# Two decoder convolutions moved under the pool, by pixel place, in column tiles; joint-step borders moved from TensorE to VectorE

## The chip, the cores and the metric

The kernel runs on one core of a Trainium2 chip. The metric is the device time of one execution in microseconds; before the change it is 17384.9 us, the median of three runs (17384.59 to 17401.33). A core has TensorE (PE, matmuls, with its weight loads shown as PEld), VectorE (DVE), ScalarE (ACT), GpSimd (POOL) and SyncE (SP), which here only issues transfers. Matmuls write to PSUM; the other tiles lie in SBUF.

## The reference, cut to what matters

A network of four residual layers on x of shape (16, 32, 128, 128) in float32. The change lies in the last one, of which this is the part that matters:

```python
def conv3x3(x, w, b): ...            # 32 -> 32 channels, zero padding 1
def maxpool2(x):
    b, c, h, w = x.shape
    return x.reshape(b, c, h // 2, 2, w // 2, 2).max(axis=(3, 5))
def deconv2x2(x, w, b): ...          # each pixel becomes a square of 2x2
orig = x
y = get_operator(x)                  # five normalised edge filters
y = conv3x3(y, conv1_w, conv1_b)     # 128x128
y = maxpool2(y)                      # 64x64
y = conv3x3(y, conv2_w, conv2_b)
y = maxpool2(y)                      # 32x32
y = conv3x3(y, conv3_w, conv3_b)
y = maxpool2(y)                      # 16x16
y = conv3x3(y, conv4_w, conv4_b)
y = deconv2x2(y, deconv1_w, deconv1_b)   # 32x32
y = conv3x3(y, conv5_w, conv5_b)
y = deconv2x2(y, deconv2_w, deconv2_b)   # 64x64
y = conv3x3(y, conv6_w, conv6_b)
y = deconv2x2(y, deconv3_w, deconv3_b)   # 128x128
y = conv3x3(y, conv7_w, conv7_b)
return orig * y
```

The layer's input is a group norm of x, and its result is added to x.

## The kernel before

The layers run one after another. The last stage is `layer3_net`; it finds the output of convolution 1, already half pooled, in DRAM (`p1`). The sixteen images form four groups; the 128 partitions hold four images of 32 channels.

**Setup.** For each of the pairs (deconvolution, convolution) 5, 6 and 7 the weights of one joint step are multiplied out on PE: `W` for the four places (phases) of a 2x2 square, a bias, and the border corrections `edge` (matmuls `pr` at L1943, then short VectorE work on one partition, L1944 to L1954). The buffers for weights are single, so a round's loads wait for the round before.

**Front of a group** (`front`). Eight loads `pt` (512 KB each, two buffers) bring p1; VectorE takes the maximum of two rows (L2053), ScalarE writes it into the padded c2 (L2055). `conv_pool` does convolutions 2 and 3: for a strip of rows nine matmuls with weights that are block diagonal over the four images (`conv9`, L354, 128 rows by 128 columns by 512 pixels) accumulate in one PSUM tile, VectorE takes the maximum over 2x2 (L1969), ScalarE adds the bias and writes the strip (L1973). Convolution 4 is one such step of 256 pixels; its result d1 goes through joint steps 5 and 6 to d2 and d3.

**Joint step.** `windows` loads, with 16 transfers from SP, one tile per image whose four groups of 32 partitions hold the same picture shifted by 0 or 1 in each direction. A matmul of 128 rows and 32 columns per image then yields one phase; the four images lie in four column tiles of PE. Joint 5 reads w5 tiles (36 KB a transfer), joint 6 w6 tiles (136 KB), joint 7 w7 tiles (528 KB). `phase` adds the border corrections with matmuls of one row: the column at L2019, and for a first or last row the row at L2025 and the corner at L2028.

**Output loop of a group.** Joint 7 for eight slices: a slice is 2048 pixels per partition. SP loads xs (1 MB), ScalarE makes xn (L2081), PE four phases, VectorE multiplies (L2088, four times) and adds xs (L2089), and ScalarE's queue stores the slice (1 MB, L2090). xs and xn have two buffers each.

The loop over groups builds the front of the next group ahead of the output loop of the current one. The order on each engine is not the program's: a scheduler fixes it at build time, engine by engine, by the expected readiness of each instruction. As built, PE runs front 0, front 1, output loop 0, front 2, output loop 1, front 3, output loops 2 and 3. SP loads w7 of a group as soon as both its d3 is written and the loop before has read the old w7; `pt` loads of the next group lie in between. The pool of PSUM tiles has seven buffers. SP's transfers carry one of eight semaphores in turn, and a transfer waits for the earlier one with the same semaphore.

Of the kernel before, what the change touches and what calls it, by code (L numbers as in the profile page):

```python
# [10 lines left out]
F32 = mybir.dt.float32  # L11
AF = mybir.ActivationFunctionType
ALU = mybir.AluOpType
AX = mybir.AxisListType
# [3 lines left out]
P = 128  # L18
B, T, HW = 16, 32, 128
# [12 lines left out]
def load(nc, pool, ap, tag):  # L32
    t = pool.tile(list(ap.shape), F32, name=tag, tag=tag)
    nc.sync.dma_start(t, ap)
    return t
# [314 lines left out]
def conv9(nc, ps, wt, src, r0, nr, nw):  # L350

    for t in range(9):
        dy, dx = divmod(t, 3)
        nc.tensor.matmul(  # L354
            ps, wt[:, t], src[:, r0 + dy : r0 + dy + nr, dx : dx + nw],
            start=(t == 0), stop=(t == 8),
        )
# [1534 lines left out]
def layer3_net(tc, w, x3, p1, out, sb3, b3, groups=range(NG)):  # L1892
# [4 lines left out]
    nc = tc.nc  # L1897
    with ExitStack() as ctx:
        cp = ctx.enter_context(tc.tile_pool(name="fc", bufs=1))
        psum = ctx.enter_context(tc.tile_pool(name="fp", bufs=7, space=PSUM))  # L1900
        psw = ctx.enter_context(tc.tile_pool(name="fpw", bufs=1, space=PSUM))
        wc = {i: load(nc, cp, w[f"c{i}_w"], f"c{i}_w") for i in range(2, 5)}
        bb = load(nc, cp, w["l3_b"], "l3_b")
        one = cp.tile([1, 64], F32, name="one", tag="one")
        nc.vector.memset(one, 1.0)


        pairs = {
            (0, 0): [(0, 1)], (0, 1): [(1, 0), (2, 1)],
# [3 lines left out]
        with tc.tile_pool(name="fw", bufs=1) as tp:  # L1913
            for i, k in ((1, 5), (2, 6), (3, 7)):
                wd = load(nc, tp, w[f"d{i}_t"], "d_t")
                bd = load(nc, tp, w[f"d{i}_b"], "d_b")
                wk = load(nc, tp, w[f"c{k}_t"], "c_t")
                pw = psw.tile([P, 4, T], F32, name="pw", tag="pw")
                for s in range(4):
                    first = True  # L1920
                    for ph in range(4):
                        rows, cls = pairs[ph // 2, s // 2], pairs[ph % 2, s % 2]
                        todo = [(dy, dx, p, q) for dy, p in rows for dx, q in cls]
                        for n, (dy, dx, p, q) in enumerate(todo):
                            nc.tensor.matmul(
                                pw[32 * s : 32 * s + 32, ph], wd[:, 2 * p + q],
                                wk[:, 3 * dy + dx, 0:T], start=first, stop=n == len(todo) - 1,
                                tile_position=(0, 32 * s), skip_group_check=True,
                            )
                            first = False  # L1930
                W = cp.tile([P, 4, T], F32, name=f"W{k}", tag=f"W{k}")
                nc.vector.tensor_copy(W, pw)

                pb = psw.tile([P, 4, T], F32, name="pb", tag="pw")
                for t in range(9):
                    nc.tensor.matmul(pb[:, 0, 0:1], wk[:, t], bd, start=(t == 0), stop=(t == 8))
                bias = cp.tile([P, 1], F32, name=f"B{k}", tag=f"B{k}")
                nc.vector.tensor_add(bias, pb[:, 0, 0:1], bb[:, k - 2 : k - 1])

                row = tp.tile([1, 3, 3, P], F32, name="row", tag="row")  # L1940
                for dy in range(3):
                    pr = psw.tile([1, 3, P], F32, name="pr", tag="pw")
                    nc.tensor.matmul(pr, bd, wk[:, 3 * dy : 3 * dy + 3], start=True, stop=True)  # L1943
                    nc.vector.tensor_scalar_mul(row[:, dy], pr, -1.0)  # L1944
                edge = cp.tile([1, 8, P], F32, name=f"E{k}", tag=f"E{k}")
                for a in range(2):
                    nc.vector.tensor_add(edge[:, a], row[:, 2 * a, 0], row[:, 2 * a, 1])
                    nc.vector.tensor_add(edge[:, a], edge[:, a], row[:, 2 * a, 2])
                    nc.vector.tensor_add(edge[:, 2 + a], row[:, 0, 2 * a], row[:, 1, 2 * a])
                    nc.vector.tensor_add(edge[:, 2 + a], edge[:, 2 + a], row[:, 2, 2 * a])  # L1950
                    for b in range(2):
                        nc.vector.tensor_scalar_mul(
                            edge[:, 4 + 2 * a + b], row[:, 2 * a, 2 * b], -1.0
                        )  # L1954
                joint[k] = W, bias, edge

        ap = ctx.enter_context(tc.tile_pool(name="fa", bufs=1))
# [1 line left out]
        sp = ctx.enter_context(tc.tile_pool(name="fs", bufs=4))  # L1959
        xp = ctx.enter_context(tc.tile_pool(name="fx", bufs=2))  # L1960

        def conv_pool(i, src, n, dst):

            nr = 512 // n
            for q in range(n // nr):
                ps = psum.tile([P, nr, n], F32, name="ps", tag="ps")
                conv9(nc, ps, wc[i], src, nr * q, nr, n)
                m = sp.tile([P, nr // 2, n // 2], F32, name="m", tag="m")
                nc.vector.tensor_reduce(  # L1969
                    m, ps.rearrange("p (y a) (x c) -> p y x a c", a=2, c=2), AX.XY, ALU.max  # L1970
                )
                r = 1 + q * nr // 2
                nc.scalar.activation(  # L1973
                    dst[:, r : r + nr // 2, 1 : 1 + n // 2], m, AF.Identity,
                    bias=bb[:, i - 2 : i - 1],
                )

        def padded(pool, n, tag):
            t = pool.tile([P, n + 2, n + 2], F32, name=tag, tag=tag)
            clear_border(nc, t, n + 2, n + 2)  # L1980
            return t
# [25 lines left out]
        def phase(k, src, n, ph, i0, nr):  # L2007

            W, bias, edge = joint[k]
            a, b = divmod(ph, 2)  # L2010
            ps = psum.tile([P, nr, n], F32, name="ps", tag="ps")
            for j in range(4):
                nc.tensor.matmul(  # L2013
                    ps[32 * j : 32 * j + 32], W[:, ph], src[j][:, i0 + a : i0 + a + nr, b : b + n],
                    start=True, stop=False, tile_position=(0, 32 * j), skip_group_check=True,
                )
            c = b * (n - 1)
            line = (a == 0 and i0 == 0) or (a == 1 and i0 + nr == n)
            nc.tensor.matmul(  # L2019
                ps[:, :, c], edge[:, 2 + b], one[:, 0:nr], start=False, stop=not line,  # L2020
                skip_group_check=True,
            )
            if line:
                r = a * (nr - 1)
                nc.tensor.matmul(  # L2025
                    ps[:, r], edge[:, a], one[:, 0:n], start=False, stop=False, skip_group_check=True
                )
                nc.tensor.matmul(  # L2028
                    ps[:, r, c : c + 1], edge[:, 4 + 2 * a + b], one[:, 0:1],
                    start=False, stop=True, skip_group_check=True,  # L2030
                )
            return ps, bias

        def joint_conv(k, src, n, dst):
# [10 lines left out]
                        nc.scalar.activation(o, ps, AF.Identity, bias=bias)  # L2045

        def front(g):
            c2 = padded(ap, 64, "c2")
            for h in range(4):
                for a in range(2):  # L2050
                    t = xp.tile([P, 2, 8, 64], F32, name="pt", tag="pt")
                    nc.sync.dma_start(t, p1[g][:, 2 * a : 2 * a + 2, 8 * h : 8 * h + 8])
                    nc.vector.tensor_tensor(t[:, 0], t[:, 0], t[:, 1], ALU.max)  # L2053
                    r = 1 + 16 * h + a
                    nc.scalar.activation(  # L2055
                        c2[:, r : r + 15 : 2, 1:65], t[:, 0], AF.Identity, bias=b3[:, g : g + 1]
                    )
            c3 = padded(bp, 32, "c3")
            conv_pool(2, c2, 64, c3)
            c4 = padded(bp, 16, "c4")  # L2060
            conv_pool(3, c3, 32, c4)
            d1 = pitched(16, "d1")
            ps = psum.tile([P, 16, 16], F32, name="ps", tag="ps")
            conv9(nc, ps, wc[4], c4, 0, 16, 16)
            nc.scalar.activation(d1[:, 1:17, 1:17], ps, AF.Identity, bias=bb[:, 2:3])
            d2 = pitched(32, "d2")
            joint_conv(5, windows(d1, 16, "w5"), 16, d2)
            d3 = pitched(64, "d3")
            joint_conv(6, windows(d2, 32, "w6"), 32, d3)
            return d3  # L2070
# [70 lines left out]
def pack(inp):  # L2141
    f = np.float32
# [106 lines left out]
    def conv(a):  # L2249
        return _diag(a.reshape(a.shape[0], a.shape[1], 9).transpose(1, 2, 0), 4)  # L2250
# [59 lines left out]
        for c in range(T):  # L2310
            selq[q, c, q, :, c] = 1.0
    w["selq"] = selq.reshape(P, 4, P)
    for n in range(2, 5):
        w[f"c{n}_w"] = conv(i[f"conv{n}_w"])
    for n in range(5, 8):
        w[f"c{n}_t"] = np.tile(i[f"conv{n}_w"].reshape(T, T, 9).transpose(1, 2, 0), (1, 1, 4))
    for n in range(1, 4):
# [24 lines left out]
```

## Time and profile before

The profiled execution took 17350.89 us, of which its span is 17349.1; the median of the runs is 17384.9.

| stage | from, us | what |
|---|---|---|
| the three layers before and the edge filters | 0 | to 16460 |
| setup of the joint weights | 16460 | 61 us |
| front 0 | 16521 | 140 us |
| front 1, output loop 0 | 16661 | 190 us |
| front 2, output loop 1 | 16851 | 191 us |
| front 3, output loop 2 | 17042 | 188 us |
| output loop 3 | 17230 | 119 us |

| engine | busy in the span, us | busy from 16460, us |
|---|---|---|
| PE | 15374.5 | 746.7 |
| DVE | 14782.1 | 247.5 |
| ACT | 12219.8 | 122.6 |
| POOL | 9818.0 | 7.1 |

A row of a profile group gives the line, engine and operation, the tiles written and read, the shapes, the number of records, the busy time, the mean of one in ns, and the idle time just before. Each float32 matmul leaves two records. The clock is the share of full TensorE speed that was granted. An engine can be busy without ending anything, so the chain of waits decides what counts.

### The profile page before, as it was taken

To read this page: it belongs to the slowest core of one execution; us is meant where nothing else is said; L and a number is where in the kernel's file an instruction comes from. 1 tells how busy PE (TensorE), PEld (TensorE's weight loads), DVE (VectorE), ACT (ScalarE), POOL (GpSimd) and SP (SyncE) were. 2 spreads that over 40 slices of the span, in tenths; PEclk is the share of its full clock that TensorE was granted. 3 is DMA by queue.
4 is the path that set the end of the run, shared out by engine and by line. 5 is a ranking of instruction groups with operands and counts; after the bars stand their busy time and mean duration, and the time that the engine had idled before them with its cause. 6 is when DMAs were issued, how large, how long until landed. Compare 5 with 4: busy or idle time off the path is not lost. (4 is left out here: it accounts for less than half of the span.)

```text
span 17349.1 us, 299637 instructions
## 1 busy us (share of the span) xinstructions
PE 15374.5 (89%) x113040; PEld 5889.8 (34%) x113040; DVE 14782.1 (85%) x14857; ACT 12219.8 (70%) x23708; POOL 9818.0 (57%) x18465
## 2 busy tenths in 40 slices
PE   8999999999999888888888888899999997688988
PEld 3333333333333322222222222255555552233433
DVE  9999999999999759999999999888888886777523
ACT  7888888888888647777777777698898882455311
POOL 9999999999999617778888888600000000000000
PEclk9999999999999989999999999898999888778888
DMA  0000000000000484444554445577777779444345
GB/s 22 12 12 12 12 12 16 12 12 12 12 13 10 70 146 155 164 161 156 166 163 163 164 161 167 158 187 198 198 196 194 198 196 206 89 77 79 72 117 177
DMA packets 1525970, 1884.46 MB, mean 109 GB/s; under 512 B 148837, under 2 KB 868765, under 8 KB 1513702
## 3 DMA queue, kind: packets, MB, share of 16 engines
q1 hardware_dynamic: 1413414, 1688.04, 37.6%
q10 hardware_dynamic: 84480, 83.91, 1.6%
q0 software_dynamic: 26624, 93.35, 1.5%
q8 instruction: 888, 14.55, 0.3%
q14 instruction: 564, 4.62, 0.1%
HBM read 1561.58 MB, written 229.64 MB: 103 GB/s over the span
## 5 line engine op out<-in xcount | busy, mean ns | idle before, releaser
L235 POOL TENSOR_SCALAR Rp<-su,nv 128x128 f32<-128x128 f32 x16384 | 5837.5, 378 | 71.7 <-PE pS L241 37.8
L224 DVE TENSOR_TENSOR Rd<-pu,nv 128x2048 f32<-128x2048 f32 x2176 | 4880.8, 2277 | 75.3 <-PE pS L241 71.6
L239 ACT ACTIVATE Ra<-su,bv 128x128 f32<-128x128 f32 x14336 | 4285.5, 388 | 540.9 <-PE pS L241 536.3
L241 PE MATMUL pS<-Rd,zw 128*32 128x512 f32 x17408 | 2907.3, 603 | 219.4 <-DVE Rd L224 219.1
L822 DVE TENSOR_TENSOR_SCAN hh<-dd,state,pd 128x512 f32<-128x512 f32 x2304 | 2823.0, 1267 | 153.7 <-PE py L856 10.6
L843 POOL TENSOR_TENSOR hh<-hh,bc 128x2048 f32<-128x2048 f32 x512 | 2319.8, 4531 | 458.4 <-DVE state L830 455.2
L241 PE MATMUL pS<-Rp,zw 128*32 128x512 f32 x8192 | 2012.3, 596 | 175.1 <-POOL Rp L235 173.2
L807 PE MATMUL pd<-du,spread 32*128 32x512 f32 x4608 | 1352.1, 661 | 571.0 <-DVE hh L822 563.1
L1228 POOL DMA_DIRECT2D x<-ob x64 | 89.4, 1396 | 3098.8 <-DVE ob L1227 2762.4
L799 ACT ACTIVATE dd<-dd,m_a 128x512 f32<-128x512 f32 x2304 | 1515.2, 714 | 339.0 <-DMA dd<-dm 328.2
L817 DVE TENSOR_TENSOR pd<-pd,bc 128x1024 f32<-128x1024 f32 x1152 | 1400.5, 1216 | 61.8 <-ACT bc L780 53.0
L241 PE MATMUL pS<-Ra,zw 128*32 128x512 f32 x7168 | 1276.2, 600 | 0.0
L1236 ACT ACTIVATE yd<-yd,nrow 128x2048 f32<-128x2048 f32 x512 | 1235.2, 2412 | 39.9 <-DMA yd<-ymap 39.9
L1116 ACT ACTIVATE ya<-pb,nrow 128x1024 f32<-128x1024 f32 x1024 | 1191.3, 1255 | 81.8 <-PE pb L1115 81.6
L1115 PE MATMUL pb<-Y,sel 32*128 32x512 f32 (+1 forms) x5120 | 1089.2, 744 | 160.6 <-ACT ya L1116 157.4
L241 PEld LDWEIGHTS pS<-Rd,zw 128*32 128x32 f32 x17408 | 623.7, 109 | 1225.2 <-issue 586.8
L807 PEld LDWEIGHTS pd<-du,spread 32*128 32x128 f32 x4608 | 373.7, 191 | 1611.6 <-DVE hh L822 717.7
L241 PEld LDWEIGHTS pS<-Rp,zw 128*32 128x32 f32 x8192 | 443.2, 109 | 1322.6 <-POOL Rp L235 863.3
L1120 DVE TENSOR_SCALAR yd<-yd 128x2048 f32<-128x2048 f32 x512 | 724.4, 1415 | 184.6 <-ACT yd L1236 183.4
L1120 DVE TENSOR_SCALAR ya<-ya 128x2048 f32<-128x2048 f32 x512 | 753.8, 1472 | 9.9 <-ACT ya L1116 8.8
L1127 PE MATMUL pd<-ya,xt 128*32 128x128 f32 x16384 | 688.7, 310 | 40.6 <-DVE ds L1280 29.6
L1127 PEld LDWEIGHTS pd<-yd,xt 128*32 128x32 f32 x16384 | 539.8, 178 | 470.2 <-issue 232.9
(421 smaller groups left out, 23716.8 us busy)
## 6 DMA issues: line engine op xcount, KB each, us to landing
dd<-dm SPq DMA_DIRECT2D x2304, 256.0 KB
yd<-ymap SPq DMA_DIRECT2D x512, 1024.0 KB
hw<-x SPq DMA_DIRECT2D x192, 512.0 KB
dm<-dt POOLq DMA_DIRECT2D x192, 256.0 KB, 3.9
xb<-tok SPq DMA_DIRECT2D x248, 144.0 KB
w<-d SPq DMA_DIRECT2D x64, 528.1 KB
x<-in_x SPq DMA_DIRECT2D x64, 512.0 KB
x<-o SPq DMA_DIRECT2D x128, 256.0 KB
```

The costliest lines, as they stand in the source:

```text
L224: nc.vector.tensor_tensor(R, st["pu"].unsqueeze(1).to_broadcast([P, 4, 4, HW]), nv[:, :, i::32].rearrange("p t q -> p q t").unsqueeze(3).t ...
L235: nc.gpsimd.tensor_scalar(R[:, q, k], su[:, k], 3.4028234e38, nv[:, k, c], ALU.min, ALU.max)
L239: nc.scalar.activation(R[:, q, k], su[:, k], AF.Relu, bias=bv[:, k, c])
L241: nc.tensor.matmul(st["pS"][32 * q : 32 * q + 32], zw[:, 31 - i : 63 - i], R[:, q], start=first, stop=False, tile_position=(0, 32 * q), sk ...
L799: S.activation(dd[:, r], dd[:, r], AF.Exp, scale=acol[:, dr, d : d + 1])
L807: nc.tensor.matmul(pd[:, a], spread[e, k], st["du"][n][e], start=True, stop=True)
L817: V.tensor_mul(pd, pd, bm.unsqueeze(1).to_broadcast([P, 2, CH]))
L822: V.tensor_tensor_scan(hh[:, r, s], dd[:, r, s], pd[:, a, s], st["state"][:, 4 * i + r : 4 * i + r + 1], ALU.mult, ALU.add,)
L843: G.tensor_mul(hh, hh, st["bc"][1, n].unsqueeze(1).to_broadcast([P, 4, CH]))
L1120: V.tensor_scalar(t, t, 1.0, 1.0, ALU.min, ALU.subtract)
L1127: M(pd[32 * q : 32 * q + 32, i], xt[:, :, xc], h, start=True, stop=True, tile_position=(0, 32 * q),)
L1236: S.activation(yd, yd, AF.Abs, bias=nrow)
```

## The change

Convolutions 2 and 3 are computed by place under the pool. c2 and c3 are kept as four planes by the parity of row and column. For each image, 16 transfers per convolution (`squares`) build a tile in which the four groups of 32 partitions hold the four planes, so that one matmul reads a 2x2 square of pixels of all channels. For each of the four places in the pool's square, four such matmuls, shifted by u and v, sum up the 3x3 filter with weights laid out for it (`c2_p`, `c3_p`, zeros where the 4x4 patch goes beyond the filter); the images are the four column tiles. ScalarE writes the first place with its bias, VectorE adds bias and takes the maximum with the other three, and `put` writes the result to the next planes. The squares use the same buffers (w6 and w5, four each) as joint steps 6 and 5. Convolution 4 is unchanged.

The border corrections of the joint steps become additions on VectorE in PSUM after the phase's matmuls; `edge` is now a column per partition, and setup makes it from the nine bias products without the `pr` matmuls.

```diff
-        wc = {i: load(nc, cp, w[f"c{i}_w"], f"c{i}_w") for i in range(2, 5)}
+        wc = {i: load(nc, cp, w[f"c{i}_p"], f"c{i}_p") for i in range(2, 4)}
+        wc4 = load(nc, cp, w["c4_w"], "c4_w")
...
-                row = tp.tile([1, 3, 3, P], F32, name="row", tag="row")
-                for dy in range(3):
-                    pr = psw.tile([1, 3, P], F32, name="pr", tag="pw")
-                    nc.tensor.matmul(pr, bd, wk[:, 3 * dy : 3 * dy + 3], start=True, stop=True)
-                    nc.vector.tensor_scalar_mul(row[:, dy], pr, -1.0)
-                edge = cp.tile([1, 8, P], F32, name=f"E{k}", tag=f"E{k}")
+                edge = cp.tile([P, 8], F32, name=f"E{k}", tag=f"E{k}")
+                nc.vector.tensor_scalar_mul(
+                    edge[:, 0:4].rearrange("p (a b) -> p a b", b=2), by[:, :, 0:3:2], -1.0
+                )
...
+        def squares(d, n, tag):
+            ts = []
+            for j in range(4):
+                t = sp.tile([P, n // 2 + 1, n // 2 + 1], F32, name=tag, tag=tag)
+                for s in range(4):
+                    nc.sync.dma_start(
+                        t[32 * s : 32 * s + 32], d[32 * j : 32 * j + 32, 1 - s // 2, 1 - s % 2]
+                    )
+                ts.append(t)
+            return ts
+
+        def conv_pool(i, src, n, put):
+            h = n // 2
+            nr = min(h, 512 // h)
+            for r in range(0, h, nr):
+                m = sp.tile([P, nr, h], F32, name="m", tag="m")
+                for ph in range(4):
+                    ps = psum.tile([P, nr, h], F32, name="ps", tag="ps")
+                    for s in range(4):
+                        u, v = divmod(s, 2)
+                        for j in range(4):
+                            nc.tensor.matmul(
+                                ps[32 * j : 32 * j + 32], wc[i][:, ph, s],
+                                src[j][:, r + u : r + u + nr, v : v + h],
+                                start=(s == 0), stop=(s == 3), tile_position=(0, 32 * j),
+                                skip_group_check=True,
+                            )
+                    b = bb[:, i - 2 : i - 1]
+                    if ph == 0:
+                        nc.scalar.activation(m, ps, AF.Identity, bias=b)
+                    else:
+                        nc.vector.scalar_tensor_tensor(m, ps, b, m, ALU.add, ALU.max)
+                put(r, m)
...
-            nc.tensor.matmul(
-                ps[:, :, c], edge[:, 2 + b], one[:, 0:nr], start=False, stop=not line,
-                skip_group_check=True,
-            )
-            if line:
+            nc.vector.tensor_scalar_add(ps[:, :, c], ps[:, :, c], edge[:, 2 + b : 3 + b])
+            if (a == 0 and i0 == 0) or (a == 1 and i0 + nr == n):
                 r = a * (nr - 1)
...
+                nc.vector.tensor_scalar_add(ps[:, r], ps[:, r], edge[:, a : a + 1])
+                o = ps[:, r, c : c + 1]
+                nc.vector.tensor_add(o, o, edge[:, 4 + 2 * a + b : 5 + 2 * a + b])
...
-            c2 = padded(ap, 64, "c2")
+            c2 = planes(ap, 64, "c2")
...
-            c3 = padded(bp, 32, "c3")
-            conv_pool(2, c2, 64, c3)
+            c3 = planes(bp, 32, "c3")
+
+            def put(r, m):
+                r //= 2
+                nr = m.shape[1] // 2
+                for a in range(2):
+                    for b in range(2):
+                        nc.scalar.copy(
+                            c3[:, a, b, a + r : a + r + nr, b : b + 16], m[:, a::2, b::2]
+                        )
+
+            conv_pool(2, squares(c2, 64, "w6"), 64, put)
             c4 = padded(bp, 16, "c4")
-            conv_pool(3, c3, 32, c4)
+            conv_pool(
+                3, squares(c3, 32, "w5"), 32, lambda r, m: nc.scalar.copy(c4[:, 1:17, 1:17], m)
+            )
```

As built from the change, SP issues in this order around the groups: the squares of c2(0), ten `pt`, the squares of c3(0), w5 and w6 of group 0; two squares of c2(1), w7(0), the other fourteen squares of c2(1), eight `pt`, the squares of c3(1), w5 and w6 of group 1; the squares of c2(2) mixed with six xs of output loop 0, w7(1), the squares of c3(2), two xs, four `pt`, w5, two `pt`, w6; the squares of c2(3) mixed with the xs of loop 1, w7(2), the squares of c3(3), two xs, w5, w6.

## The prediction

> **What bounds the kernel.** The page's span is 17349.1 us and its first row gives PE 89%, but the touched code is only the last network stage. I found its start in the chain of waits, at 16460 us, so it has 889 us (5%); nothing before it changes. I then cut the stage into its groups with the busy times by window (start:end, length, then PE, PEld, DVE, ACT, POOL busy, PE clock, DMA share, GB/s):
>
> ```profile
> 16460.00:16521.00 61.00, 35.25 (x288) 22.50 (x288) 15.19 (x54) 5.00 (x4) 0.68 (x6) 0.52 0.27 93
> 16521.00:16661.00 140.00, 125.30 (x350) 54.74 (x350) 20.93 (x31) 18.89 (x32) 1.73 (x18) 0.90 0.27 81
> 16661.00:16851.00 190.00, 170.54 (x687) 69.86 (x686) 52.10 (x60) 24.32 (x30) 2.12 (x21) 0.92 0.55 149
> 16851.00:17042.00 191.00, 171.62 (x690) 70.81 (x690) 55.37 (x62) 30.51 (x33) 2.12 (x21) 0.92 0.57 165
> 17042.00:17230.00 188.00, 166.99 (x686) 69.31 (x686) 56.85 (x59) 27.08 (x26) 0.45 (x3) 0.93 0.55 155
> 17230.00:17349.10 119.10, 76.99 (x336) 24.26 (x336) 47.06 (x45) 16.76 (x8) 0.00 (x0) 0.74 0.75 225
> ```
>
> Setup, front 0, three periods (a front and the output loop of the group before it), and the last output loop. The chain of waits inside one period (start, length, what) says what ends each part:
>
> ```profile
> 16851.47 79.19 PE ps L354 x180
> ...
> 16938.55 1.89 DMA w<-d
> ...
> 16958.52 15.85 PE ps L2013 x44
> ...
> 16996.23 7.37 DMA out<-xn
> 17003.63 8.24 DMA out<-xn
> 17011.98 9.71 DMA out<-xn
> ```
>
> 79 us of convolutions 2 and 3 on PE (180 records are two per fp32 matmul, so 90 matmuls of 860 ns), then window loads and joint steps, then an output loop that stores pace, one per 8 us, not PE. The PE groups by shape for the stage (records, busy, mean ns, idle before):
>
> ```profile
> L354 PE MATMUL ps<-c,c_w 128*128 128x512 f32 x720 | 314.6, 599 | 3.3 <-ACT c L2055 3.3
> L2013 PE MATMUL ps<-w,W 128*32 128x512 f32 x1280 | 270.4, 665 | 75.0 <-DMA w<-d 47.1 <-DVE xn L2088 27.8
> L2019 PE MATMUL ps<-one,E 1*128 1x8 f32 x256 | 52.9, 277 | 0.0
> ```
>
> Last, what the DMA engines do while PE convolves. Windows cut where the loads of w7 (16 DMAs of 528 KB, 8.65 MB) begin and end, and after them:
>
> ```profile
> 16662.00:16706.00 44.00, 44.00 (x104) 19.45 (x103) 3.46 (x5) 2.02 (x5) 0.00 (x0) 1.00 0.96 197
> 16706.00:16740.00 34.00, 32.62 (x77) 14.05 (x75) 3.46 (x5) 3.24 (x7) 0.86 (x8) 1.00 0.00 0
> 16851.00:16901.00 50.00, 50.00 (x115) 22.24 (x115) 10.49 (x12) 4.51 (x7) 0.00 (x0) 0.96 0.95 217
> 16901.00:16931.00 30.00, 29.65 (x70) 12.72 (x68) 2.32 (x4) 2.43 (x5) 0.72 (x8) 1.00 0.00 0
> ```
>
> So w7 takes 44 us alone and 50 beside the last stores, with the DMA engines 95% busy. Today the 79 us of PE hide it. That cover is what the change takes away.
>
> **PE's own gain.** Convolution 2 goes from 72 matmuls of 128x512 to 128 in four column tiles. Column tiles of joint step 7 do overlap: in the timeline its four run in 1.06 us, and start 1.31 us apart with a 0.39 us edge row between. So 128/4 x 0.86 = 27.5 us against 72 x 0.86 = 62; convolution 3 64/4 x 0.43 = 6.9 against 15.5. That is 43 us a group, 172 in all, if nothing else became late. Evacuation does not bind: per PSUM tile of 3.44 us one VectorE pass (0.82, the row of L2088) or ScalarE's (0.73), and four copies of 128 elements at 0.40 (L1973) per half.
>
> **What becomes late: the windows.** Both convolutions now need 16 window DMAs from SP, of the shapes that joint 6 (136 KB) and joint 5 (36 KB) load already. From those rows: source ready to first PE work 4.6 us (16629.4 to 16634.0) and to the last window 12.9 (16642.3); for the small ones 3.9 and 11.7. Where windows arrive singly the laid-out order gives PE seven matmuls of each of the first three tiles before the fourth's second; matmuls of one tile do not overlap. Joint 6 shows it: the 22 matmuls of `x44` take 15.9 us, where full overlap would take 5 and their windows' arrival 8. Then the fourth tile runs its 32 one after another: 17 x 0.86 + 27.5 = 42 us from the first window, not 27.5. For convolution 3 it is 16 x 0.43 = 7 after the last window.
>
> I place these along SP's new order. "d1" is convolution 4's evacuation.
>
> - Front 0. Setup loses nine `pr` matmuls with their row copies (5.8 us in each of three rounds, two of them gating the next load): E is ready near 16502, not 16520. The other six `pt` loads take 18.7 us as today (16520.9 to 16539.6), so c2 is whole at 16523 (today PE starts on its first rows), first window 16527.7, +42 and 2 for a slow PE clock = 16572, evacuated 16575, +11.7 +8 = 16595, +1.5 +5.8 +0.5: d1 at 16602 against 16612. **-10.**
> - Front 1. SP issues two of c2's squares, then all of w7 for group 0, then the other 14. From T1 = 16661.9 (d3 written) w7 takes 44, so PE, which today starts at once, starts at T1+44.5; +42 +2 = 88.6, +2.7, +11.7 +8 = 111, +1.5 +4: d1 at T1+117 against T1+82.7 (16744.6). **+34.** The `pt` loads that sit in its joint steps today move forward (52.6 us against 49.8 in front 0): -3.
> - Fronts 2 and 3. Their convolution 2 has its squares during the output loop and runs at once from T0 (16851.5), 27.5 us. But convolution 3's squares stand behind w7 on SP, which ends at T0+50; eight semaphore slots and 0.63 us an issue bring the last at T0+57.5; +7 +1. ScalarE has the next two xn (they wait for 2 MB of xs behind those squares) ahead of c4's copy: T0+69. d1 at T0+75 and T0+73.5 against 85.2 and 83.5. **-10 each**; in front 2 `pt` loads before w5 take 1 back.
>
> **Edges.** The K=1 matmuls become VectorE additions in PSUM: a group has 44 columns, 12 rows and 12 corners, 272 instructions in all. No small in-place PSUM operation is in the trace. Near rows: 0.16 us (128x1 from PSUM, L1938), 0.17 (128x8, L1841), 0.28 (1x128, L1947). Ends 0.16 and 0.5; I take 0.19, as most are short. In joint 6 the eight steps of 1.3 to 1.7 us become eight of 0.86 with a longer VectorE tail: -4.2; in joint 5 -1. So **-5.2 a front**, -21. In the output loop four columns, 0.8 us a slice (an eighth of a group), lie in VectorE's wait for xn (2 to 4.8 us before each slice): nothing; without that cover 32 x 0.8 = 26. In the last loop seven tiles come before the first product, at half clock: +2. At 0.5 us an instruction the slice's 2 us would still fit the wait; the joint tails would give back about half of the 21.
>
> **Small parts.** VectorE loses 40 reductions of 0.69 and gains 36 passes of 0.5 to 0.82: it idles there. ScalarE writes c2 in 64 pieces of about 0.5 for 32 of 0.73; GpSimd clears plane borders in pieces of 0.1 to 0.2. All lie beside PE or DMA: nothing, except some 2 us in front 0, held in the doubts below.
>
> **Output loops.** ScalarE issues store q after xn(q+1), which waits for store q-1: stores are serial. SP mixes 14 to 16 squares among the xs loads of loops 0 and 1 (0.28 MB on 2 MB a slice), while some `pt` leave. Bounds 0 and +1.1 us a slice (by bytes); I take +2 a loop: **+4**.
>
> **Sum.** -10 +34 -3 -10 -9 -10 -21 +2 +4 = -23. PE restarts at half clock after a wait (0.50 in 5 us windows at 16955 and 17275), and the change adds about four waits beyond those priced; at 2 to 3 us each I add 10: **-13 us** on 17349.1. The medians lie 34 us above that execution (17384.9 against 17350.9), so 17372.
>
> **Rule against row.** The Trainium skill, "DMA: Bandwidth & Descriptors", section "Where 436 GB/s comes from", lets SBUF-to-SBUF copies reach 435 GB/s; an estimate from it is 20 us for w7. The rows have 197 to 217. By the rule front 1 would wait 24 less and convolution 3 of fronts 2 and 3 would not wait at all (d1 at T0+58, 16 earlier each): -69. The measured row decides.
>
> **Rivals.**
> - *Faster:* w7 gates less (faster, or squares landing beside it). For it: PE's 172 us. Against: 95% DMA share. By the sum above 17316.
> - *Slower:* squares among the xs loads hold SP's queue (0.63 us each, plus slots held by stores), so the store chain of loops 0 and 1 goes from 8.0 to 11.5 us: 16 x 3.5 - 4 - 13 = +39, 17424. It decides from 3.3 us a slice. For: stores are serial and SP is in order. Against: xs is loaded two ahead, and 14% more bytes explain 1.1.
> - *The change does not do what it says:* column tiles with K=128 in accumulation do not overlap: 128 x 0.86 + 64 x 0.43 = 138 us against 77.5, some +240. Joint 7's 1.06 us speaks against.
>
> **Numbers.** Measurement tells 0.2% (35 us) from no change. Chances: my sum 0.48, faster rival 0.37, slower 0.13, no overlap 0.02; so faster 0.37, same 0.48, slower 0.15. Range 17300 (the faster case with cheaper fronts) to 17424; my case alone 17340 to 17400.
>
> **What would show it.** PE idle some 44 us before front 1's convolution 2 and 20 or more before convolution 3 of fronts 2 and 3, ended by DMA of w from c: right. A convolution 2 in fronts 2 and 3 far from 27.5 us, a w7 shorter than 40, corrections over 0.3 us, or stores over 9 us apart would each make a term wrong.

## The result and the profile after

The changed kernel takes 17349.5 us (median of 20 runs), the kernel before, run in turn with it, 17398.3. The ratio is 0.9973, 95% interval 0.9962 to 0.9985: 47 us less, between 26 and 66. So the kernel is faster by 0.27%, a little more than the 0.2% that I took a measurement to tell from nothing (the near end of the interval, 0.15%, lies below it), and by 34 us more than I forecast.

The profiled execution of the changed kernel is no help as a whole: it took 17413.6 us (span 17411.8), 63 us *more* than that of before. But its first matmul into pw, where the touched code begins, starts at 16585.1 us against 16471.3, and nothing before that point was changed in what it computes. In a second profile of the same changed kernel it starts at 16422.0. So everything below compares the **stage from the first pw matmul to the end**: 877.8 us before, 826.7 after (828.3 in the second profile). Those 51 us agree with the 47 of the ratio.

Cut into its parts by the same marks in each trace, in us (d1 and d3 are the ends of their last writes, and the number behind them is the group; a "period" runs from d3 of one front to d1 of the next and contains an output loop and the convolutions of that next front; "my parts" are the forecast terms that fall into the row, without the 10 us that I held back for restarts):

| part | before | after | difference | my parts |
|---|---|---|---|---|
| first pw to d1(0): setup, front 0 | 140.8 | 120.4 | -20.4 | -10 |
| d1 to d3, joint steps 5 and 6, four times | 199.4 | 170.6 | -28.8 | -24 |
| d3(0) to d1(1), front 1 | 82.7 | 112.8 | +30.1 | +34 |
| two periods, d3(1) to d1(2) and d3(2) to d1(3) | 280.6 | 253.8 | -26.8 | -15 |
| d3(3) to the end, output loops 2 and 3 | 174.3 | 169.1 | -5.2 | +2 |
| stage | 877.8 | 826.7 | -51.1 | -13 |

The windows of the new profile, cut near the same events (start:end, length, busy time of PE, PEld, DVE, ACT and POOL, PE clock, DMA share, GB/s): setup, front 0, front 1 with output loop 0, the next two periods, the last loop.

```profile
16574.00:16635.00 61.00, 23.97 (x283) 22.91 (x282) 10.10 (x38) 11.41 (x18) 1.83 (x21) 0.54 0.41 137
16635.00:16747.00 112.00, 88.86 (x498) 30.77 (x498) 20.75 (x53) 15.78 (x36) 1.88 (x18) 0.87 0.36 99
16747.00:16954.00 207.00, 120.64 (x754) 40.37 (x758) 56.97 (x123) 28.36 (x44) 2.82 (x25) 0.80 0.59 159
16954.00:17124.00 170.00, 111.65 (x760) 38.66 (x754) 63.84 (x130) 30.59 (x39) 1.67 (x17) 0.84 0.70 196
17124.00:17290.00 166.00, 107.82 (x754) 48.52 (x750) 59.97 (x125) 25.43 (x27) 0.45 (x3) 0.83 0.60 174
17290.00:17411.80 121.80, 58.33 (x260) 14.30 (x256) 54.28 (x90) 18.85 (x9) 0.00 (x0) 0.75 0.76 236
```

PE is busy 50 to 60 us less in each of the three middle rows, but the third row is 17 us longer than its 190 of before and the next two only some 20 shorter. Where the rest is, PE's timeline shows (start, length, line, shapes, records, and in brackets the idle time before and what ended it), first front 1 before, then fronts 1 and 2 after:

```profile
16661.05 77.53 PE L354 MATMUL ps<-c,c_w 128*128 128x512 f32 x180
```

```profile
16793.32 40.96 PE L1998 MATMUL ps<-w,c_p 128*32 128x512 f32 x256 [47.95 <-DMA w<-c]
...
16954.18 29.53 PE L1998 MATMUL ps<-w,c_p 128*32 128x512 f32 x256
17005.35 1.89 PE L1998 MATMUL ps<-w,c_p 128*32 128x256 f32 x4 [21.64 <-DMA w<-c]
```

Before, front 1's convolutions 2 and 3 ran at once, in 77.5 us. Now its convolution 2 stands still for 48 us until its squares land, and then takes 41; front 2's runs at once and takes 29.5, but its convolution 3 waits 21.6 (25.4 in front 3). SP's timeline says what stands ahead of the squares (L1980; four transfers an image, 16 in all): w7 (L2033), with 37 and 43 us of issue.

```profile
16744.63 1.14 SPq L1980 DMA_DIRECT2D w<-c  x2
16747.10 37.39 SPq L2033 DMA_DIRECT2D w<-d  x16
16784.53 13.40 SPq L1980 DMA_DIRECT2D w<-c  x14
...
16954.42 42.56 SPq L2033 DMA_DIRECT2D w<-d  x16
16997.09 14.07 SPq L1980 DMA_DIRECT2D w<-c  x16
```

### The profile page after: what moved, and what is told of

The parts are those of the page before. It is cut to its first block, busy times and chain, and to the rows that moved or that the text cites. A ratio compares the mean times of both kernels' runs of the same rounds, so it can differ in the third digit from the quotient of the medians.

```text
span 17411.8 us, 300873 instructions
## 1 busy us (share of the span) xinstructions
PE 15201.4 (87%) x113294; PEld 5760.5 (33%) x113294; DVE 14898.3 (86%) x15100; ACT 12226.0 (70%) x23748; POOL 9787.4 (56%) x18465
## 5 line engine op out<-in xcount | busy, mean ns | idle before, releaser
L235 POOL TENSOR_SCALAR Rp<-su,nv 128x128 f32<-128x128 f32 x16384 | 5807.8, 395 | 142.2 <-PE pS L241 108.5
L241 PE MATMUL pS<-Rp,zw 128*32 128x512 f32 x8192 | 1937.0, 596 | 145.3 <-POOL Rp L235 140.7
```

What stands on the lines that cost most here:

```text
L235: nc.gpsimd.tensor_scalar(R[:, q, k], su[:, k], 3.4028234e38, nv[:, k, c], ALU.min, ALU.max)
L241: nc.tensor.matmul(st["pS"][32 * q : 32 * q + 32], zw[:, 31 - i : 63 - i], R[:, q], start=first, stop=False, tile_position=(0, 32 * q), sk ...
```

## The experiments

All ten runs by part, in us of their profiled execution (the ratio is to the kernel before, run beside them; "joints" is the sum of four):

| run | to d1(0) | joints | d3(0)-d1(1) | d3(1)-d1(2) | d3(2)-d1(3) | d3(3)-end | stage | ratio (95%) |
|---|---|---|---|---|---|---|---|---|
| before | 140.8 | 199.4 | 82.7 | 141.5 | 139.1 | 174.3 | 877.8 | |
| after | 120.4 | 170.6 | 112.8 | 126.7 | 127.1 | 169.1 | 826.7 | 0.9973 (0.9962-0.9985) |
| after again | 120.4 | 170.5 | 112.9 | 126.4 | 127.9 | 170.3 | 828.3 | 0.9973 (0.9964-0.9982) |
| convolutions alone | 138.2 | 197.5 | 113.9 | 130.9 | 130.2 | 175.2 | 885.9 | 1.0007 (0.9995-1.0019) |
| corrections alone | 121.6 | 171.8 | 81.9 | 136.4 | 135.1 | 170.4 | 817.1 | 0.9967 (0.9956-0.9979) |
| squares on GpSimd | 121.4 | 173.9 | 86.4 | 124.3 | 142.2 | 173.7 | 821.8 | 0.9968 (0.9940-0.9995) |
| w7 on GpSimd | 120.1 | 172.6 | 100.0 | 145.4 | 130.9 | 175.0 | 844.1 | 0.9983 (0.9968-0.9997) |
| front 1 block diagonal | 119.1 | 170.9 | 81.9 | 167.3 | 125.5 | 169.8 | 834.6 | 0.9984 (0.9973-0.9995) |
| corrections twice | 120.3 | 181.7 | 112.4 | 125.4 | 126.1 | 172.1 | 838.0 | 0.9975 (0.9965-0.9985) |
| squares before w7 | 118.3 | 173.6 | 71.2 | 126.8 | 133.5 | 172.6 | 795.9 | 0.9962 (0.9950-0.9973) |
| own buffers, early pt | 120.5 | 172.0 | 69.7 | 132.3 | 118.3 | 168.7 | 781.5 | 0.9950 (0.9933-0.9966) |
| w7 in halves | 120.9 | 189.5 | 54.2 | 113.8 | 105.1 | 169.9 | 753.3 | 0.9932 (0.9920-0.9945) |

### The two halves of the change, one at a time

The convolutions by place with the border matmuls and the setup of before (the hunks of `phase` and of `edge` taken back):

```diff
-            nc.vector.tensor_scalar_add(ps[:, :, c], ps[:, :, c], edge[:, 2 + b : 3 + b])
+            nc.tensor.matmul(
+                ps[:, :, c], edge[:, 2 + b], one[:, 0:nr], start=False, stop=not line, ...
```

> The convolutions by place are in, the border corrections stay matmuls on PE and the setup stays as before. Compared over the stage from the first matmul into pw to the end: 877.8 us before, 826.7 after. If the corrections on VectorE earn what the trace of after suggests (some 32 us in the joint steps, 9 in the output loops, and the 17 us of setup), the convolutions alone earn nothing: about 875. If my prediction's smaller terms for the corrections hold (21 us and nothing in the loops) and the convolutions were better than I summed: about 850.

And the other half: the corrections on VectorE with their setup, and `conv9` under `conv_pool` as before:

```diff
-                            nc.tensor.matmul(
-                                ps[32 * j : 32 * j + 32], wc[i][:, ph, s], ...
+                conv9(nc, ps, wc[i], src, nr * q, nr, n)
```

> The border corrections on VectorE and their setup are in, the convolutions stay block diagonal with nine matmuls. If the corrections carry the gain: each joint pair (from d1 to d3) 8 us shorter, 42 instead of 50, output loops 3 shorter each, front 0 earlier by part of the 17 us of setup; stage about 825 to 830, as short as with both parts. If the corrections are worth only what I predicted: joints 45, loops unchanged, stage about 850.

The convolutions alone give 885.9 us and a ratio of 1.0007: nothing, or 8 us lost. The corrections alone give 817.1, as short as both or shorter, and 0.9967. The parts add up: +8 and -61 make -53, the change measured -51. **The small-looking half carries all of the gain**; the half with 172 us of PE time in it pays +31 in front 1 and earns 11 and 9 in the two periods. The intervals of "corrections alone" and "after" overlap; that it is the faster kernel is shown by one profile's stage only.

Where the corrections earn is seen in three places. The first is the setup: that of before (PE's timeline), then that of the corrections alone:

```profile
16475.12 3.99 PE L1936 MATMUL pb<-d_b,c_t 32*128 32x1 f32 x18 [0.38 <-DVE W L1932]
16479.36 1.43 PE L1943 MATMUL pr<-c_t,d_b 32*1 32x384 f32 x2 [0.25 <-DVE B L1938]
...
16487.92 3.45 PE L1925 MATMUL pw<-c_t,d_t 32*32 32x32 f32 x72 [2.99 <-issue]
```

```profile
16596.69 3.99 PE L1937 MATMUL pb<-d_b,c_t 32*128 32x1 f32 x18 [0.38 <-DVE W L1932]
16603.88 3.45 PE L1925 MATMUL pw<-c_t,d_t 32*32 32x32 f32 x72 [3.20 <-DMA c_t<-in_c_t]
```

From one pb to the next pw took 12.8 us and takes 7.2; that comes twice, and the `pr` matmuls of the last round go too, so that front 0 begins 18.4 us sooner (PE starts convolution 2 50.3 us after the first pw before, 31.9 with the corrections alone).

The second is the joint steps, 27.6 us in all. PE's timeline of joint step 6 in front 0, before and then in the changed kernel:

```profile
16633.99 15.98 PE L2013 MATMUL ps<-w,W 128*32 128x512 f32 x44 [5.15 <-DMA w<-d]
...
16650.65 1.05 PE L2013 MATMUL ps<-w,W 128*32 128x512 f32 x2
...
16652.38 1.05 PE L2013 MATMUL ps<-w,W 128*32 128x512 f32 x2
```

```profile
16724.98 20.39 PE L2046 MATMUL ps<-w,W 128*32 128x512 f32 x64 [6.20 <-DMA w<-d]
```

Before, behind the first 16 us, the matmuls of a phase come 1.3 to 1.7 us apart, with the border matmuls between, and the last ends 27.1 us after the first began. After, all 64 records take 20.4 us.

The third is the start of an output loop. In loops 0 to 2 its first store leaves 9.6, 9.8 and 8.5 us after d3 before, and 5.6, 5.6 and 5.5 after. The corrections do this: alone they give 5.7, 5.7 and 5.5, and the convolutions alone 8.6, 8.6 and 8.5. PE and VectorE together (weight loads left out), before and then after, just behind d3(1):

```profile
16795.88 1.06 PE L2013 MATMUL ps<-w,W 128*32 128x512 f32 x8
16795.99 0.96 DVE L2088 SCALAR_TENSOR_TENSOR xn<-ps,B,xn 128x512 f32<-128x512 f32 x1 [0.31 <-PE ps L2028]
16796.87 0.38 PE L2019 MATMUL ps<-one,E 1*128 1x8 f32 x2
16797.12 0.41 PE L2025 MATMUL ps<-one,E 1*128 1x64 f32 x2
16797.37 0.33 PE L2028 MATMUL ps<-one,E 1*128 1x1 f32 x2
16797.63 1.07 PE L2013 MATMUL ps<-w,W 128*32 128x512 f32 x8
16797.74 0.96 DVE L2088 SCALAR_TENSOR_TENSOR xn<-ps,B,xn 128x512 f32<-128x512 f32 x1 [0.79 <-PE ps L2028]
```

```profile
16902.09 0.75 DVE L2126 SCALAR_TENSOR_TENSOR xn<-ps,B,xn 128x512 f32<-128x512 f32 x1
...
16903.30 2.14 DVE L2126 SCALAR_TENSOR_TENSOR xn<-ps,B,xn 128x512 f32<-128x512 f32 x3
16905.32 0.25 DVE L2051 TENSOR_SCALAR ps<-ps,E 128x8 f32<-128x8 f32 x1
16905.47 2.29 DVE L2127 TENSOR_TENSOR xn<-xn,xs 128x2048 f32<-128x2048 f32 x1
```

Before, a phase of the first slice comes from PE every 1.3 to 1.75 us, edges included, and VectorE waits for each. After, PE has run ahead in the seven PSUM tiles while joint step 6 was being written, and VectorE takes the phases back to back.

### The corrections made twice

```diff
-            nc.vector.tensor_scalar_add(ps[:, :, c], ps[:, :, c], edge[:, 2 + b : 3 + b])
+            for _ in range(2):      # edge holds half the value
+                nc.vector.tensor_scalar_add(ps[:, :, c], ps[:, :, c], edge[:, 2 + b : 3 + b])
...
```

> As the changed kernel, but every border correction is made twice, with half the value, so that VectorE has 272 more instructions of about 0.2 us, 54 us in all. If they lie beside other work in the output loops, the loops stay as they are (stores 7.8 us apart, first store 5.6 us after d3) and only the joint steps 5 and 6 grow, by at most 28 x 0.2 = 5.6 us a front and probably 1 to 2: stage 831 to 850. If the corrections are on the path of the output loops, each slice grows by 0.8 us: another 26 us, stage 860 or more.

838.0: the joint steps grow by 11.1 us in all, 2.8 a front. The last part, two loops paced by stores, grows by 3 for 80 more additions (16 us), and 2 of these 3 are the first store of loop 2, which leaves 7.5 us after d3 and not 5.5. The periods don't grow: the first stores of loops 0 and 1 leave 2 us later too, but convolution 2 of the next front starts 52.7 and 51.6 us after d3, against 52.0 and 51.4 in the changed kernel. So in the output loops nearly all of the additions lie in VectorE's wait, as I had priced them, but for the first slice; in the joint steps half of their time (11 of 112 x 0.2 = 22) is on the path. The rows of VectorE by shape in this run (count, busy, mean ns):

```profile
L2052 DVE TENSOR_SCALAR ps<-ps,E 128x8 f32<-128x8 f32 x256 | 43.1, 226 | 48.5 <-PE ps L2046 48.3
L2057 DVE TENSOR_TENSOR ps<-ps,E 128x1 f32<-128x1 f32 x96 | 14.5, 157 | 0.2
L2055 DVE TENSOR_SCALAR ps<-ps,E 128x64 f32<-128x64 f32 x32 | 8.3, 282 | 0.1
```

### Is it SP's order, or the engines?

The squares issued by GpSimd instead of SP, and, in another kernel, w7 instead:

```diff
-                    nc.sync.dma_start(
+                    nc.gpsimd.dma_start(
                         t[32 * s : 32 * s + 32], d[32 * j : 32 * j + 32, 1 - s // 2, 1 - s % 2]
```

> As the changed kernel, but the squares are issued by GpSimd, not SP, so that they no longer stand behind w7 in SP's order; the bytes are the same. Theory of the queue: the convolution 2 of front 1 starts 13 to 20 us after d3 instead of 47, convolution 3 of fronts 2 and 3 starts 10 us or more earlier (T0+40 instead of T0+51), w7 gets longer by the squares' bytes (44 to some 50); stage about 780. Theory of the engines (w7 keeps them 95% busy, so squares beside it crawl wherever they are queued): convolution 2 of front 1 still starts past T1+35 and the stage stays near 820.

```diff
-                    nc.sync.dma_start(
+                    (nc.gpsimd if n == 64 else nc.sync).dma_start(
                         t[32 * s : 32 * s + 32].rearrange("p r c -> p (r c)"),
```

> As the changed kernel, but the 16 loads of w7 are issued by GpSimd and all else stays on SP. Theory of the queue: as with the squares moved, stage about 780, and the xs loads no longer stand behind w7 either, so convolution 4 of fronts 2 and 3 is not late by xn. Theory of the engines: near 820.

Both theories hold in part, and the stage follows neither: 821.8 and 844.1. PE's timeline with the squares on GpSimd, front 1 and then front 3:

```profile
16681.28 11.81 PE L1998 MATMUL ps<-w,c_p 128*32 128x512 f32 x28 [7.29 <-DMA w<-c]
16695.93 7.86 PE L1998 MATMUL ps<-w,c_p 128*32 128x512 f32 x14 [2.84 <-DMA w<-c]
16708.77 29.84 PE L1998 MATMUL ps<-w,c_p 128*32 128x512 f32 x214 [4.98 <-DMA w<-c]
...
17028.98 12.78 PE L1998 MATMUL ps<-w,c_p 128*32 128x512 f32 x28 [1.19 <-DMA w<-c]
17047.68 7.88 PE L1998 MATMUL ps<-w,c_p 128*32 128x512 f32 x14 [5.93 <-DMA w<-c]
17062.75 30.34 PE L1998 MATMUL ps<-w,c_p 128*32 128x512 f32 x214 [7.19 <-DMA w<-c]
```

In front 1 (d3 written at 16675.7) the first window is there after 5.6 us instead of 46, the last only after 33: the squares left at once, but share the DMA engines with w7 (from 16676 to 16712 both together move 215 GB/s, against 200 while w7 alone went ahead in the changed kernel). GpSimd's own issuing is not what holds them: the sixteenth was issued 12 us after d3, and in front 0 of this run, with no w7 beside them, convolution 2 takes 41.5 us behind GpSimd's squares as behind SP's. d1(1) comes 26 us sooner. Front 3 shows the same picture, where there was no wait before: the pt loads that fill its c2 had been placed behind the windows of joint 6, so that its squares left only when w7 did. That costs 15 us there. With w7 on GpSimd front 1 gains 13 us, but the first period grows by 19, through VectorE. Its timeline there, beside w7:

```profile
16974.39 0.74 DVE L2008 SCALAR_TENSOR_TENSOR m<-ps,l_b,m 128x512 f32<-128x512 f32 x1
17009.35 0.69 DVE L2078 TENSOR_TENSOR pt<-pt 128x512 f32<-128x512 f32 x1 [34.23 <-DMA pt<-p]
17009.96 0.75 DVE L2008 SCALAR_TENSOR_TENSOR m<-ps,l_b,m 128x512 f32<-128x512 f32 x1
```

The maxima of pt (L2078, for the next group) were mixed into those of convolution 2 (L2008); a pt load that SP had issued by 16974 landed only at 17009, beside w7. VectorE stood 34 us before it, and c3 was whole only at 17034 although PE had done its 28 us of convolution 2 by 16993. So the wait is made by order, but freeing it moves the collision to the next transfer that meets w7.

### Front 1 as before

```diff
-                d3 = front(groups[n + 1])
+                d3 = front(groups[n + 1], n == 0)   # True: block diagonal, nine matmuls, no squares
```

> As the changed kernel, but the front of the second group (the one that the changed kernel makes 30 us longer) does its convolutions 2 and 3 as before: block diagonal, nine matmuls, no squares; its weights are loaded as well. If the parts add up by fronts (convolutions by place: front 0 -1, front 1 +31, fronts 2 and 3 -10 and -8), d3(0) to d1(1) goes back from 113 to 82 us and nothing else moves: stage 796. If the 31 us in front 1 are work that w7 must do anyway and that comes back elsewhere (w7 and the first output loop late), the stage stays above 815.

A miss: 834.6 and not 796. Front 1 went back to 81.9, as expected; but the next period grew from 126.7 to 167.3. PE and then SP of this run:

```profile
16868.89 38.45 PE L1999 MATMUL ps<-w,c_p 128*32 128x512 f32 x242 [43.99 <-DMA w<-c]
```

```profile
16817.57 43.41 SPq L2056 DMA_DIRECT2D w<-d  x16
16861.03 10.04 SPq L1981 DMA_DIRECT2D w<-c  x10
```

Ten of the sixteen squares of c2(2) now stood behind w7(1): the pt loads that fill c2 were placed behind windows of front 1's joint steps, where the changed kernel has them ahead. The 31 us are not tied to front 1; they fall to whichever front's squares meet w7 on SP.

### Taking the wait away

Three steps, each built on what the one before had shown; their edits are shown shortened. First w7 behind the squares of c2 on SP, c3's squares on GpSimd:

```diff
+            s2 = squares(c2, 64, "w6", nc.sync)
+            if d is not None:
+                w7 = windows(d, 64, "w7")        # each ordered behind the last square
...
-                3, squares(c3, 32, "w5"), 32,
+                3, squares(c3, 32, "w5", nc.gpsimd), 32,
```

> As the changed kernel, but SP issues all 16 squares of c2 ahead of w7, and the squares of c3 go through GpSimd; buffers as in the change. By the theory that the wait in front 1 is the order of SP: convolution 2 starts 6 us after d3(0) instead of 46, d3(0) to d1(1) 75 to 85 us instead of 113; convolution 3 of fronts 2 and 3 starts at T0+42 instead of T0+51, 10 us each. Stage 765 to 785. If what SP no longer holds back comes late in another place (pt of the next group behind the joint windows, as with all squares on GpSimd), one of the fronts 2 and 3 gets longer by 10 to 35 us and the stage stays near 800 or more.

Front 1 takes 71.2 us, better than expected (convolution 2 starts 2.3 us after d3). Convolution 3 of fronts 2 and 3 waits 10 and 11 us instead of 22 and 25, but their squares of c2 now come late, behind late pt again: convolution 2 takes some 40 us there, and front 3 gets 6 longer. The stage is 795.9, between the two expectations. Then, in one step, buffers of their own for c2's squares and pt placed early:

```diff
-            s2 = squares(c2, 64, "w6", nc.sync)
+            s2 = squares(c2, 64, "s6", nc.sync)
+            c2 = inputs(nxt)                     # pt loads and c2 of the next group
```

> As the one before, and the squares of c2 have buffers of their own (m has two instead of four to make room), so that they need not wait for joint step 6, and the pt loads of the next group are placed right behind the squares of c2, ahead of w7. Convolution 2 of each front then finds all its windows: 28 us, no gap, at once after d3(0) in front 1. d3(0) to d1(1) 64 to 70 us instead of 113; d3(1) to d1(2) and d3(2) to d1(3) about 110 instead of 127. Stage about 745; if the engines are full and the transfers only change places (xs late for the first slice, w7 late for the output loop), 790 or more.

781.5, again between the two. Convolution 2 now takes 28 to 29 us in fronts 1 to 3 without a gap, but convolution 3 still waits 12, 22 and 10 us for its first window, and from the end of convolution 2 to that of convolution 3 it takes 39, 44 and 31 us. The theory was that its squares share the engines with w7. So w7 was cut:

```diff
-                w7 = windows(d, 64, "w7")
+                w7 = windows(d, 64, "w7", range(2))                       # SP, behind c2's squares
+                w7 += windows(d, 64, "w7", range(2, 4), nc.gpsimd)        # behind c3's squares
```

> As the version with own buffers and early pt, but w7 is loaded in two halves: two of its four tiles by SP behind the squares of c2, the other two by GpSimd behind the squares of c3, so that these no longer share the engines with the second half. By the theory that the gaps left before convolution 3 (12 to 22 us in fronts 1 to 3 of the version before) are w7's transfers beside the squares: the gaps shrink to 5 to 8 us, d3(0) to d1(1) 58 to 62 us instead of 69.7, d3(1) to d1(2) 110 to 118 instead of 132.3, d3(2) to d1(3) about 110 instead of 118.3; stage 745 to 760. Rival: the second half then stands beside the windows of joint steps 5 and 6 or comes late for the output loop, which gives the gain back: stage 775 or more.

753.3, and 0.9932 (0.9920 to 0.9945), the fastest of all: by the ratio 118 us less than before, by the stage 124.5. PE's timeline, convolutions 2 and 3 of front 1, then convolution 3 of fronts 2 and 3:

```profile
16594.12 28.03 PE L1998 MATMUL ps<-s,c_p 128*32 128x512 f32 x247
16633.90 12.03 PE L1998 MATMUL ps<-w,c_p 128*32 128x256 f32 x128 [11.74 <-DMA w<-c]
...
16795.56 12.29 PE L1998 MATMUL ps<-w,c_p 128*32 128x256 f32 x128 [15.84 <-DMA w<-c]
...
16950.10 1.78 PE L1998 MATMUL ps<-w,c_p 128*32 128x256 f32 x4 [5.01 <-DMA w<-c]
```

The waits for the first window are 11.7, 15.8 and 5.0, not all the 5 to 8 expected; but the later windows no longer come singly, and from the end of convolution 2 to that of convolution 3 it takes 24, 28 and 18 us, 13 to 16 less each. So the theory holds in its main. In front 2 SP began the first half of w7 only 20 us before the squares left (16764.2 and 16784.6), so they may have met its end; this was not tested further. The rival was right in part: the joint steps got 5 to 8 us longer in fronts 1 to 3 (48.2, 50.1, 48.6), where the second half of w7 stands beside their windows. The stage is what was expected.

### The changed kernel again

> The changed kernel once more, beside the version with w7 in halves on the same chip, to see how far one execution's stage differs from another's: stage 826.7 us in the first profile; parts d3(0) to d1(1) 112.8, d3(1) to d1(2) 126.7, d3(2) to d1(3) 127.1, joint pairs 41.6 to 43.5. If a single profile carries the reading, each part comes back within 2 us and the stage within 5.

Every part comes back within 1.2 us, the stage within 1.6. As far as one repeat can tell, one profile carries the reading of a part, and what varies lies ahead of the stage: its first pw starts 163 us earlier in this execution.

## Why the prediction was right and where it was not

The direction and the range were right; the size was not: 13 us forecast, 51 in the stage. Two errors lay in opposite directions. **The line of the sum has one -10 too many**: the parts above it (front 0 -10, front 1 +34 -3, fronts 2 and 3 -9 and -10, edges -21, +2, +4) make -13, and with the 10 held back for restarts the text should have said -3. So the parts were 48 us from the truth, not 38.

That the range held is in part luck. I gave "no change" the better chance (0.48, "faster" 0.37), and the only way to "faster" that I had priced, a w7 that gates less, did not occur. Sorted by the two halves, my parts give the corrections -37 (setup -18, joint steps -21, loops +2) and the convolutions +24; alone they measure -61 and +8. So I had the signs right and both halves too slow, the corrections most.

- **What becomes late** was right, step by step. Front 1: PE idle 48 us before convolution 2 (forecast 44), and the part grows by 31 with the convolutions alone (+34). In the changed kernel it takes 19.7 us from the end of convolution 2 to the end of convolution 3, where I had summed 22.4. The -3 for `pt` rested on a wrong reading: the joint steps of front 1 took 50.5 us before, not 52.6, against 49.8 in front 0. Fronts 2 and 3, counted from the start of their convolution 2 (T0): PE idle 21.6 and 25.4 us before convolution 3 (forecast 20 or more), and d1 at T0+74.6 and T0+75.7 (75 and 73.5). With the late fourth window convolution 2 takes 41.0 to 41.5 (42), with all windows 28.2 to 29.5 (27.5).
- **The row against the rule** on w7: over PE's 46 us of waiting in front 1 (16747 to 16793; w7, and the squares behind it) the DMA engines are 97% busy at 200 GB/s, as in the profile before. The Trainium skill's 435 GB/s ("DMA: Bandwidth & Descriptors", "Where 436 GB/s comes from") was not reached by these loads, each of which fills 32 partitions; what holds them at half of it no run here shows. Choosing the row was right, and the rival built on the rule is out. So are the other two: stores of loops 0 and 1 stand 7.9 and 8.2 us apart, and four column tiles overlap.
- **Front 0, -10 forecast, -20.4 measured.** That the `pr` rounds go was summed right (E 18 us sooner; the corrections alone bring 19.2). The term that was mis-sized is what the convolutions by place would give back there, 8 us: alone they give back nothing and bring 2.6. Their first window came 53.5 us after the first pw (forecast 56.4), although the six pt loads took the 18.7 us that I had taken from before: they began 1.6 us sooner, and the window followed the last write of c2 after 3.4 us and not 4.7. Convolution 2 took 41.5 and not 44, from its end to convolution 3's end 19.6 and not 22.7, and from there to d1 5.8 and not 7.8.
- **Edges in the joint steps, -21 forecast, -27.6 with the corrections alone.** The price of an addition was right (54.5 us for 272, 0.20 each, against 0.19). The shorter PE time was mis-sized: in the changed kernel joint 5 of front 0 is 2.3 shorter instead of 1, joint 6 6.0 instead of 4.2.
- **Edges in the output loop, "nothing" and +2.** This was the step in kind that failed. I asked what the additions would cost VectorE, and that is hidden but for the first slice, as the doubled ones show. I did not ask what taking the matmuls off PE gives: the first slice of a loop has no store ahead of it and was bound by PE, so in loops 0 to 2 it leaves 3 to 4 us sooner. With the corrections alone convolution 2 of fronts 2 and 3 then starts 4.2 and 4.5 us sooner after d3, and the two periods and the last part change by -5.1, -4.0 and -3.9: 13 us less where I had 2 more.
- **Output loops, +4.** With the convolutions alone convolution 2 of fronts 2 and 3 starts 55.4 and 55.7 us after d3, against 56.3 and 55.4 before. The squares among xs cost nothing, the lower of my two bounds.
- **The 10 us for slow restarts** do not appear as a sum of their own. PE does restart slowly: in front 1 the first five records of convolution 2 start 0.84 us apart, the later ones of one tile 0.43. But I had already added 2 to 4 us at each wait that I priced, and the parts leave no room for more.

## What to carry to other kernels

Time taken off an engine is worth only what the work behind it can start sooner. Here 172 us of PE bought nothing as long as the inputs that it then needed stood behind a larger transfer, while some short matmuls were worth 61 us because others waited for just these, in the setup, the joint steps and the first slice of a loop. When a change adds small transfers that an engine waits for, look which big one is ahead of them in their queue and how much slack that one has; then order the big one behind the small, and split it so that it doesn't share the engines with them. Here moving either to another queue alone only chose another transfer to be late (821.8 and 844.1 us, against 753.3).

## What the hardware showed that I had not expected

- A second queue is no priority. With the squares on GpSimd beside w7, the last window was there 33 us after d3, against 13 for transfers of this size alone (joint 6 before): a share of the engines, not a place ahead.
- The last column tile to get its input sets the end. With windows coming one by one within 13 us, convolution 2 takes 41 us; with all windows there, 28.0. A tile runs its own matmuls one after another, 32 x 0.86 = 27.5 us, and the fourth tile begins them only when its window lands: 27.7 us from the first moment with all four at work to the end in front 1, 29.8 with the squares on GpSimd. What the other three tiles did ahead of it saved nothing.
- Small additions in PSUM cost far less than in proportion to their width: 0.16 us for one column, 0.23 for 8 or 16, 0.28 for 64.
